# Router tokens turned by transfers and VectorE, token stores ahead of the slots' part, and a new written-out order

## The chip, the cores and the metric

The kernel runs on one core of one Trainium2 chip. The metric is the device time of one execution in microseconds (us); for the kernel before it is the median of three runs. All data are fp32. TensorE is called PE (its weight loads PEld), VectorE DVE, ScalarE ACT, GpSimd POOL, and the queue that issues most transfers SP.

## What is computed

The input x is 32 sequences of 512 tokens of 256 features. Two blocks follow each other, both with a residual.

- Attention: x is normalised; from it come a charge q (one number per token, tanh), a shell vector (64, scaled to length 1) and values. cos and sin of a projection of the shell, times the powers q^0 to q^4, are combined into phi (64). The weights are softmax(phi phi^T times a decay by distance), causal; x becomes x + weights @ values @ W_out.
- Slots (the feed-forward part), on the x that attention left:

```
xm    = layernorm(x)
h     = gelu(xm @ w1x.T + (part of the slots' mean) + b1)
alpha = softmax over the 8 largest of (h @ w2.T + b2), 0 for the other 56 slots
gi    = sum over tokens of alpha * xm / sum of alpha        # one row per slot
S'    = GRU(gi, slots)                                      # 64 slots per sequence
out   = x + alpha @ (S' @ wv.T + bv) @ wo.T + bo
```

## The kernel before, in words

The 32 sequences are taken two at a time: 16 groups of 2 sequences, of 8 token tiles of 128 tokens. For each group the code records steps (`add`): an engine, a cost, a function that emits the instructions, the steps it comes after, and the buffers it uses. Nothing is emitted while recording. At the end `Plan.order` places all steps of all groups one by one: it gives each a rank (from its place along the group's chain, the group's number times `STRIDE`, and a `DELAY` for each stage) and takes the step that could start first by the recorded costs, with the lower rank first among equals. Steps of several groups are mixed in this way. Each engine then runs its instructions strictly in that written-out order, SP's and POOL's transfers too. `SLOTS_OF` says how many buffers of each kind there are (x: 5 buffers of 8 tiles).

The stages of a group, with the lines of the kernel before:

1. load: `load_x` loads the tokens x twice, once as tokens (2 transfers of 512 KB) and, from group 2 on, once in 32x32 blocks as xb (8 transfers of 128 KB, L276).
2. tokens: `columns` turns xb into xT on DVE (L843, four 32x32-block transposes per group; groups 0 and 1 by PE, L821); `statistics` (DVE L753, POOL L764 to L774); `project` (PE L873) gives pf, DVE L886 scales it into sv.
3. angles: charges, shells, then five products tp: sine on ACT (L1042), two multiplications on DVE and two on POOL (`power`, all of them L1053).
4. phi (PE L1073, DVE L1088), then for the tiles (0,1), (2), (3): logits (PE L1127), their smallest with the mask (DVE L1156), exponent (ACT L1168), the weights turned (PE L1205, ACT L1223), values (PE L1211), and the sum onto x in place (DVE L1240).
5. normal: `statistics` again (POOL takes about 4 us for its part), xm on ACT (L1263, eight instructions of 128x256). `transposed` turns xm: 16 PE transposes of 128x128 (L789) into PSUM, four ACT copies of 128x512 out of it (L801).
6. router: hidden (PE L1290), gelu (ACT L1301), logits (PE L1315, turned in L1321), the 8 largest (DVE L1346 and L1347, eight times), softmax, al (POOL L1380).
7. taken, gru: psi (PE L1404), gi, the GRU's gates (PE L1454), small steps on DVE, ACT and POOL.
8. given: alpha turned (PE L1525), values of the slots (PE L1542), py (PE L1562). DVE adds py onto x in place (L1576, four of 128x512), and SP stores the tile pairs (L1581, four transfers of 256 KB). Until then the group holds its x buffer.

Of the kernel before, what the change touches and what calls it, by code (L numbers as in the profile page):

```python
# [15 lines left out]
P = 128  # L16
D = 256
# [6 lines left out]
SQ = 32  # L24
BY_TENSOR = 2
SHELL = 64
# [28 lines left out]
    "x": 5,  # L55
    "xb": 2,
    "xT": 4,
    "xmT": 4,
# [8 lines left out]
    "row": 8,  # L67
    "half": 5,
# [3 lines left out]
HOP = 0.28  # L72
TABLE = 1.28
SWITCH = 0.78
STRIDE = 36.18
LATE = 0.64
# [3 lines left out]
    "load": (14.7, 32.3),  # L80
    "tokens": (-16.4, 4.9),
    "angles": (-28.4, -6.2),
    "phi": (36.8, 9.6),
    "weights": (6.0, -2.0),
    "values": (-3.0, -21.2),
    "normal": (-19.3, -7.3),
    "router": (38.2, 2.0),
    "taken": (14.1, 0.1),
    "gru": (-28.5, -3.9),
    "given": (10.5, 2.0),  # L90
# [152 lines left out]
def block_kernel(ctx: ExitStack, tc: tile.TileContext, a: dict, out: bass.AP):  # L243
# [46 lines left out]
    def load_x(g, after=()):  # L290
        xs[g] = lazy("x", f"x_{g}", [P, GT, D])
        x_in[g] = []
        for bb in range(GB):

            def dst(g=g, bb=bb):
                return xs[g]()[:, bb * NT : (bb + 1) * NT, :]

            x_in[g].append(
                load("SP", dst, x[g * GB + bb].rearrange("(c p) d -> p c d", p=P), 512, after, [xs[g]])
            )  # L300
        if g < BY_TENSOR:
            return
        for bb in range(GB):
            xb = xbs[g, bb] = lazy("xb", f"xb_{g}_{bb}", [P, T // SQ, KD * SQ])
            blocks = x[g * GB + bb].rearrange("(t i) (q e) -> q i t e", i=SQ, q=P // SQ)
            xb_in[g, bb] = [
                load(
                    "SP",
                    lambda q=q, xb=xb: xb()[q * SQ : (q + 1) * SQ, :, :],
                    blocks[q],  # L310
                    128,
                    after,
                    [xb],
                    rate=150.0,
                )
                for q in range(P // SQ)
            ]
# [32 lines left out]
    xms = [const(f"xm{i}", [P, GT, D + 1]) for i in range(SLOTS_OF["xm"])]  # L350
# [165 lines left out]
    for q in range(P // SQ):  # L516
# [102 lines left out]
    def make_mask():  # L619
# [17 lines left out]
        lambda: [nc.gpsimd.memset(xm[:, :, D : D + 1], 1.0) for xm in xms],  # L637
# [6 lines left out]
    l_w1x = load("SP", w1x, rows(a["w1_t"][0:D, :]), 128, rank=30.0)  # L644
    l_w1s = load("SP", w1s, rows(a["w1_t"][D : 2 * D, :]), 128, rank=30.0)
# [133 lines left out]
    def transposed(g, n, src, uses, after, tag):  # L779

        res = {}
        for bb in range(GB):
            for k in range(KD):
                pt = bank(f"pt{n}_{g}_{bb}_{k}")
                dst = lazy(tag, f"{tag}_{g}_{bb}_{k}", [P, T])

                def turn(bb=bb, k=k, pt=pt):
                    for c in range(NT):
                        nc.tensor.transpose(  # L789
                            pt()[:, c * P : (c + 1) * P],  # L790
                            src()[:, bb * NT + c, k * P : (k + 1) * P],
                            ident,
                        )

                s = add(
                    "PE", 0.44, turn, after[bb * NT : (bb + 1) * NT] + [s_ident], uses + [pt, dst]
                )
                s = add(
                    "ACT",
                    0.54,  # L800
                    lambda dst=dst, pt=pt: nc.scalar.copy(dst(), pt()),  # L801
                    [s],
                    [pt, dst],
                )
                res[bb, k] = (dst, s)
        return res

    def columns(g, xt):
# [3 lines left out]
        for bb in range(GB):  # L812
# [25 lines left out]
            else:  # L838
                for h in range(2):
# [12 lines left out]
                    done.append([add("DVE", 0.6, turn, xb_in[g, bb], [xbs[g, bb], dst])])  # L852
# [3 lines left out]
    def features(g):  # L856
# [9 lines left out]
        for t in range(GT):  # L866
# [4 lines left out]
            def project(c=c, pf=pf, tile_=tile_):  # L871
                for k in range(KD):
# [12 lines left out]
                    0.42,  # L885
# [40 lines left out]
        qb = lazy("row", f"qb_{g}", [P, T])  # L926
        q2 = lazy("row", f"q2_{g}", [P, T])

        def charges_turned():
# [7 lines left out]
        s = add("PE", 0.44, charges_turned, s_rep + [s_ident], [qrep, ptq, qb])  # L937
        s_qb = add(
            "ACT", 0.6, lambda: nc.scalar.activation(qb(), ptq(), AF.Tanh), [s], [ptq, qb], "exp"
        )  # L940
        s_q2 = add(
            "ACT", 0.6, lambda: nc.scalar.activation(q2(), qb(), AF.Square), [s_qb], [qb, q2]
# [58 lines left out]
        tp = small(f"tp_{g}", [P, ORDER + 1, T], bufs=1)  # L1001
# [30 lines left out]
        def nearest():  # L1032
# [5 lines left out]
        s_tp = {}  # L1038
        s_tp[0] = add(
            "ACT",  # L1040
            0.6,
            lambda: nc.scalar.activation(tp()[:, 0, :], turn(), AF.Sin, scale=-TWO_PI),  # L1042
            [s],
            [turn, tp],
            "sin",
        )

        def power(eng, cost, m, by, s_by):
            e = nc.vector if eng == "DVE" else nc.gpsimd
            s_tp[m] = add(  # L1050
                eng,
                cost,
                lambda: e.tensor_tensor(  # L1053
                    tp()[:, m, :], tp()[:, m - 1 if by is qb else m - 2, :], by(), ALU.mult
                ),
                [s_tp[m - 1 if by is qb else m - 2], s_by],
                [tp, by],
            )

        power("DVE", 0.75, 1, qb, s_qb)  # L1060
        power("POOL", 1.2, 2, q2, s_q2)
        power("DVE", 0.75, 3, q2, s_q2)
        power("POOL", 1.2, 4, q2, s_q2)
# [4 lines left out]
        def combined():  # L1068
# [13 lines left out]
            "PE", 2.3, combined, list(s_tp.values()) + [s_wc], phs + [tp, phi], split="64x64"  # L1082
# [19 lines left out]
    def attention(g, sv, s_sv, phi, s_phi):  # L1102
# [147 lines left out]
        return s_x  # L1250

    def router(g, s_x):

        xt = xs[g]
        plan.stage = "normal"
        xm = Lazy("xm", lambda: xms[g % len(xms)])
        al = lazy("al", f"al_{g}", [P, NT, GB, SLOTS])
        ln, s_ln = statistics(g, "b", xt, [xt], s_x)
        s_xm = [
            add(  # L1260
                "ACT",
                0.51,
                lambda t=t: nc.scalar.activation(  # L1263
                    xm()[:, t, 0:D],
                    xt()[:, t, :],
                    AF.Identity,
                    bias=ln()[:, 4, t : t + 1],
                    scale=ln()[:, 1, t : t + 1],
                ),
                [s_ln, s_one],  # L1270
                [xm, xt, ln],
            )
            for t in range(GT)
        ]
        xm_t = transposed(g, "b", xm, [xm], s_xm, "xmT")
# [7 lines left out]
        for bb in range(GB):  # L1283
            ph = bank(f"ph_{g}_{bb}")
            h_t = lazy("h_t", f"h_t_{g}_{bb}", [H, T])
            tiles = [xm_t[bb, k][0] for k in range(KD)]

            def hidden(ph=ph, tiles=tiles):
                for k in range(KD):
                    nc.tensor.matmul(  # L1290
                        ph(), w1x[:, k, :], tiles[k](), start=(k == 0), stop=(k == KD - 1)
                    )

            s = add(
                "PE", 1.72, hidden, [xm_t[bb, k][1] for k in range(KD)] + [l_w1x], tiles + [ph, h_t]
            )
            s_h.append(
                add(
                    "ACT",
                    0.6,  # L1300
                    lambda ph=ph, h_t=h_t: nc.scalar.activation(h_t(), ph(), AF.Gelu, bias=b1e),  # L1301
                    [s, s_b1e],
                    [ph, h_t],
                    "gelu",
                )
            )
            h_ts.append(h_t)
# [35 lines left out]
        for t in range(GT):  # L1343
# [5 lines left out]
            s_top.append(add("DVE", 0.38, taken, [s], [rl, rest, top]))  # L1349
# [40 lines left out]
        return xm, al, s_al  # L1390

    def slots(g, xm, al, s_al):
# [7 lines left out]

        def taken_in():
            for c in range(NT):
                for bb in range(GB):
                    nc.tensor.matmul(  # L1404
                        psi()[bb * SLOTS : (bb + 1) * SLOTS, 0 : D + 1],
                        al()[:, c, bb, :],
                        xm()[:, bb * NT + c, :],
                        start=(c == 0),
                        stop=(c == NT - 1),
                    )  # L1410

        def amounts():
            nc.vector.tensor_scalar(rw(), psi()[:, D : D + 1], 1e-8, None, ALU.add)
# [3 lines left out]
        s_gi = add(  # L1417
            "DVE", 0.38, lambda: nc.vector.tensor_copy(gi(), psi()[:, 0:D]), [s_psi], [psi, gi]
        )
# [133 lines left out]
        )  # L1553
        for c2 in range(NT // 2):
# [15 lines left out]
            s = add("PE", 0.95, given, [s_val, s_alt], pys + [al_t, val], split="64x128")  # L1570
            for bb in range(GB):
                t = bb * NT + 2 * c2
# [7 lines left out]
                def stored(bb=bb, c2=c2, t=t):  # L1580
# [8 lines left out]
                add("SP", 0.8, stored, [s_y], [xt], land=2.0)  # L1589

    for g in range(NG):
# [6 lines left out]
        s_x = attention(g, sv, s_sv, phi, s_phi)  # L1598
        xm, al, s_al = router(g, s_x)
        slots(g, xm, al, s_al)  # L1600
# [63 lines left out]
```

## Time and profile before

| what | us |
|---|---|
| median of 3 runs (lowest, highest) | 727.66 (727.29, 728.21) |
| profiled execution, its own time | 729.78 |
| span in the profile, first to last instruction | 728.0 |
| one group in the even middle of the span (start of L1073 of one group to that of the next) | 42.27 |

The profile is of one execution, so its own time, 729.78, lies 2.1 us above the median; what is worked out from it is a difference, and is taken off the median. In the profile's rows a group of instructions is given by line, engine, operation, out<-in, sizes and count, then busy time, mean ns of one and idle time before. PE instructions are pipelined: the time that one takes on the engine is the distance from its start to the next one's start, which is shorter than its printed duration (a 128x128 transpose: 109 ns apart, 276 ns long). DVE instructions overlap likewise, by some 70 ns.

In the first 46 us PE is idle for 11.4 us (loads and weights), in the last 45 us for 13.7 us; between them it is idle for 4.8 us in all.

### The profile page before, as it was taken

The page shows a single profiled execution, that of the slowest core. Times are in us where ns is not written, and L with a number is a line of the kernel's source. Part 1 is how long each engine was busy: PE and PEld are TensorE (multiplying, and loading weights), DVE is VectorE, ACT ScalarE, POOL GpSimd, SP SyncE. Part 2 cuts the span into 40 slices and gives each one's busy share as a digit, 9 for nine tenths or more (in the row PEclk, how much of TensorE's full clock was granted, in tenths as well). Part 3 has the DMA queues.
Part 4 walks back from the last instruction along what each step waited for, and adds up shares of the span by engine and source line. Part 5 has one row for each costly group of instructions (what it writes and reads, how often), then busy time and mean ns, then how long its engine had stood idle before and what let it go on. Part 6 is the DMA issues. An engine that isn't in the chain of part 4 may idle for free.

```text
span 728.0 us, 12427 instructions
## 1 busy us (share of the span) xinstructions
PE 698.1 (96%) x4170; PEld 484.4 (67%) x4170; DVE 598.6 (82%) x1747; ACT 419.8 (58%) x866; POOL 268.3 (37%) x510
## 2 busy tenths in 40 slices
PE   4989999999999999999999999999999999999975
PEld 3747675777676767667676766767677667667443
DVE  3889978699797979889797988979797968768574
ACT  2335666846484765647476564747656582967631
POOL 6361624244151624425152442515243433231220
PEclk9999999999999999999999999999999999999989
DMA  6865422033333041333304123330410301000113
GB/s 143 265 119 140 73 45 59 1 117 59 116 58 117 8 109 59 59 117 59 116 14 103 59 59 116 59 116 21 97 58 1 116 1 59 1 1 1 58 43 132
DMA packets 99151, 53.76 MB, mean 74 GB/s; under 512 B 63088, under 2 KB 98256, under 8 KB 99088
## 3 DMA queue, kind: packets, MB, share of 16 engines
q1 hardware_dynamic: 97216, 52.02, 28.0%
q0 software_dynamic: 496, 0.33, 0.4%
q8 instruction: 33, 0.54, 0.3%
q10 hardware_dynamic: 1376, 0.62, 0.3%
q14 instruction: 30, 0.25, 0.1%
HBM read 35.85 MB, written 16.78 MB: 72 GB/s over the span
## 4 chain that ended last, share of the span: by engine, by line
PE 62%; DVE 27%; ACT 3%; POOL 3%; DMA 2%; issue 2%; SPq 1%; ACTq 0%; DVEq 0%; POOLq 0%
PE po L1211 15%; PE ph L1290 7%; DVE sv L886 6%; PE ptp L1205 5%; PE pl L1127 5%; PE prz L1454 4%; PE pf L873 4%; PE py L1562 4%; PE pph L1073 4%; DVE rest L1347 3%; DVE bnb L753 3%; DVE x L1240 3%; PE psi L1404 2%; PE prr L1315 2%; PE pv L1542 2%; DVE top L1346 2%
## 5 line engine op out<-in xcount | busy, mean ns | idle before, releaser
L1211 PE MATMUL po<-sv,prT 128*128 128x256 f32 x640 | 148.6, 381 | 1.1 <-DVE nm L1156 1.1
L1211 PEld LDWEIGHTS po<-sv,prT 128*128 128x128 f32 x640 | 116.8, 189 | 18.5 <-ACT prT L1223 1.3
L873 PE MATMUL pf<-wfb,xT 128*128 128x321 f32 x448 | 125.6, 436 | 0.0
L873 PEld LDWEIGHTS pf<-wfb,xT 128*128 128x128 f32 x448 | 83.3, 189 | 38.0 <-issue 4.5
L1263 ACT ACTIVATE xm<-x,lnb 128x256 f32<-128x256 f32 x128 | 64.6, 587 | 29.6 <-POOL lnb L774 29.6
L1168 ACT ACTIVATE pr<-lg,nm 128x512 f32<-128x512 f32 (+3 forms) x128 | 70.9, 555 | 7.4 <-DVE nm L1156 5.9
L1053 POOL TENSOR_TENSOR tp<-tp,q 128x512 f32<-128x512 f32 x32 | 48.9, 1528 | 68.8 <-ACT tp L1042 67.5
L1240 DVE SCALAR_TENSOR_TENSOR x<-po,den,x 128x256 f32<-128x256 f32 x128 | 60.2, 474 | 13.5 <-PE po L1211 13.1
L764 POOL TENSOR_TENSOR lnb<-bnb 128x8 f32<-128x8 f32 x16 | 3.3, 208 | 179.0 <-DVE bnb L753 179.0
L1156 DVE CUSTOM_DVE_ANT_0 lg<-pl,mask 128x512 f32<-128x512 f32 (+3 forms) x128 | 57.0, 484 | 9.1 <-PE pl L1127 8.6
L886 DVE SCALAR_TENSOR_TENSOR sv<-pf,lna,bias_f 128x321 f32<-128x321 f32 x128 | 62.0, 538 | 2.7 <-POOL lna L770 2.5
L1290 PE MATMUL ph<-xmT,w1x 128*128 128x512 f32 x128 | 60.9, 602 | 0.0
L1364 ACT ACTIVATE rl<-rl,rtau 128x512 f32<-128x512 f32 x16 | 11.6, 723 | 83.1 <-DVE rl L1355 83.1
L1576 DVE TENSOR_TENSOR x<-py,x 128x512 f32<-128x512 f32 x64 | 39.9, 683 | 21.3 <-PE py L1562 21.3
L753 DVE BATCH_NORM_STATS2 bnb<-x 128x6 f32<-128x256 f32 x128 | 54.1, 426 | 3.7
L1223 ACT COPY prT<-ptp 128x384 f32<-128x384 f32 (+1 forms) x96 | 46.1, 513 | 18.1 <-PE ptp L1205 18.1
L753 DVE BATCH_NORM_STATS2 bna<-x 128x6 f32<-128x256 f32 x128 | 47.1, 413 | 6.9 <-DMA x<-in_x_dram 6.9
L1205 PE MATMUL ptp<-ident,pr 128*128 128x128 f32 x320 | 46.7, 277 | 0.0
L1127 PE MATMUL pl<-phi 64*128 64x256 f32 (+1 forms) x384 | 46.4, 364 | 0.0
L1205 PEld LDWEIGHTS ptp<-ident,pr 128*128 128x128 f32 x320 | 36.3, 140 | 13.7 <-issue 6.0
L1073 PE MATMUL pph<-tp,wc 64*64 64x256 f32 x640 | 38.9, 381 | 0.2 <-POOL tp L1053 0.2
L1127 PEld LDWEIGHTS pl<-phi 64*128 64x128 f32 x384 | 30.3, 186 | 12.4 <-issue 8.9
(177 smaller groups left out, 1338.3 us busy)
## 6 DMA issues: line engine op xcount, KB each, us to landing
x<-in_x_dram SPq DMA_DIRECT2D x32, 512.0 KB, 5.1
out_dram<-x SPq DMA_DIRECT2D x64, 256.0 KB, 2.5
xb<-in_x_dram SPq DMA_DIRECT2D x112, 128.0 KB, 3.5
setup<-in_gru_whh_t_dram SPq DMA_DIRECT2D x1, 768.0 KB, 5.7
wih<-in_gru_wih_t_dram SPq DMA_DIRECT2D x1, 768.0 KB, 6.8
wfb<-wf SPq DMA_DIRECT2D x8, 40.1 KB, 5.2
setup<-in_W_v_dram ACTq DMA_DIRECT2D x1, 256.0 KB, 9.0
setup<-in_W_out_t_dram ACTq DMA_DIRECT2D x1, 256.0 KB, 9.0
```

The lines of the kernel that those rows point to most:

```text
L753: lambda t=t: nc.vector.bn_stats(st()[:, t, :], src()[:, t, :]),
L873: nc.tensor.matmul(pf()[:, 0:NF], tile_()[:, k, c * P : (c + 1) * P], w[:, k, :], start=(k == 0), stop=(k == KD - 1),)
L886: lambda t=t, pf=pf: nc.vector.scalar_tensor_tensor(sv()[:, t, :], pf()[:, 0:NF], ln()[:, 1, t : t + 1], bias_f, ALU.mult, ALU.add,),
L1073: nc.tensor.matmul(phs[h]()[bb * COMB : (bb + 1) * COMB, 0:HT], wc[r, m, :], tp()[r, m, bb * HT : (bb + 1) * HT], start=(m == 0), stop=(m ...
L1127: nc.tensor.matmul(pls[bb]()[:, off[i] + lo : off[i] + lo + w], phi()[r, 0, q : q + P], phi()[r, 1, k : k + w], start=True, stop=True,)
L1156: nc.vector.tensor_tensor_reduce(out=lg()[:, c], in0=pls[bb]()[:, c], in1=mask[:, T - w : T], scale=1.0, scalar=TOP, op0=ALU.add, op1=ALU.min,
L1168: nc.scalar.activation(pr()[:, c], lg()[:, c], AF.Exp, bias=nm(), scale=-1.0, accum_out=den()[:, tiles.index(i), bb : bb + 1],)
L1205: nc.tensor.transpose(pt()[:, j : j + P], prs[bb]()[:, j : j + P], ident)
L1211: nc.tensor.matmul(po()[:, d * D : (d + 1) * D], pr_t()[:, lo : lo + P], sv()[:, bb * NT + j, C_V:NF], start=(j == 0), stop=(j == i),)
L1240: nc.vector.scalar_tensor_tensor(xt()[:, t, :], po()[:, d * D : (d + 1) * D], den()[:, d, bb : bb + 1], xt()[:, t, :], ALU.mult, ALU.add,)
L1263: lambda t=t: nc.scalar.activation(xm()[:, t, 0:D], xt()[:, t, :], AF.Identity, bias=ln()[:, 4, t : t + 1], scale=ln()[:, 1, t : t + 1],),
L1290: nc.tensor.matmul(ph(), w1x[:, k, :], tiles[k](), start=(k == 0), stop=(k == KD - 1))
```

## The change

- Router tokens: for groups 0 to 13 the 16 PE transposes and four ACT copies go. xm is laid out as [128, 4 quarters of 64 features, 8 tiles, 64 + 1]; 32 transfers by SP (16 per sequence, each of 32 partitions x 1,040 bytes, SBUF to SBUF) put blocks where they belong, and four DVE transposes in 32x32 blocks finish it, in place (xmT). The hidden matmul reads the new layout with rows of w1 in another order (w1b, four more loads at the start); gelu writes its output back into the order of tokens. Groups 14 and 15 turn by PE as before.
- Stores: for groups 0 to 14, SP stores x (2 transfers of 512 KB) as soon as attention is done. ACT copies py out of PSUM into ys (four of 128x512), and POOL issues two transfers of 512 KB that add ys onto what was stored. DVE's four additions of 128x512 go. Group 15 is as before.
- Powers: two DVE multiplications of 128x1024 take the place of two of 128x512 on DVE and two on POOL; q and q^2 lie in the same tile.
- Buffers: x 5 to 4, xT 4 to 3, xmT 3 of another shape, row 8 to 6, half 5 to 4; new: ys 2.
- Ranks: `HOP`, `SWITCH`, `STRIDE`, `LATE`, every `DELAY` and some costs have new values, so the written-out order is another one on every engine.

```diff
-    "x": 5,
+    "x": 4,
...
+    "ys": 2,
+    "row": 6,
+    "half": 4,
...
-HOP = 0.28
+HOP = 0.41
-SWITCH = 0.78
-STRIDE = 36.18
-LATE = 0.64
+SWITCH = 1.41
+STRIDE = 11.97
+LATE = 0.85
...
-    "normal": (-19.3, -7.3),
-    "router": (38.2, 2.0),
-    "taken": (14.1, 0.1),
-    "gru": (-28.5, -3.9),
-    "given": (10.5, 2.0),
+    "normal": (-37.6, -17.2),
+    "router": (-0.8, -0.4),
+    "taken": (-20.0, -22.0),
+    "gru": (4.0, 0.6),
+    "given": (-0.8, -23.8),
...
-        power("DVE", 0.75, 1, qb, s_qb)
-        power("POOL", 1.2, 2, q2, s_q2)
-        power("DVE", 0.75, 3, q2, s_q2)
-        power("POOL", 1.2, 4, q2, s_q2)
+        for m in (1, 3):
+
+            def powers(m=m):
+                a, b = tp()[:, 0:1, :], tp()[:, ORDER + 1 : ORDER + 3, :]
+                if m == 1:
+                    a = a.to_broadcast([P, 2, T])
+                else:
+                    a, b = tp()[:, 1:3, :], b[:, 1:2, :].to_broadcast([P, 2, T])
+                nc.vector.tensor_tensor(tp()[:, m : m + 2, :], a, b, ALU.mult)
+
+            s_tp.append(add("DVE", 1.3, powers, [s_tp[-1], s_q], [tp]))
...
+        if g < NG - LAST_BY_VECTOR:
+
+            for bb in range(GB):
+
+                def store(bb=bb):
+                    nc.sync.dma_start(
+                        out=out[g * GB + bb].rearrange("(c p) d -> p c d", p=P),
+                        in_=xt()[:, bb * NT : (bb + 1) * NT, :],
+                    )
+
+                stored.append(
+                    add("SP", 1.7, store, s_x[bb * NT : (bb + 1) * NT], [xt], land=3.0)
+                )
...
+                moved = [
+                    add(
+                        "SP",
+                        0.45,
+                        lambda bb=bb, q=q, b=b, dst=dst: nc.sync.dma_start(
+                            out=dst()[q * SQ : (q + 1) * SQ, b * NT : (b + 1) * NT, :],
+                            in_=xm()[b * SQ : (b + 1) * SQ, q, bb * NT : (bb + 1) * NT, :],
+                        ),
+                        here,
+                        [xm, dst],
+                        land=2.3,
+                    )
+                    for b in range(NT)
+                    for q in range(NQ)
+                ]
+                for h in range(2):
+
+                    def turn(h=h, dst=dst):
+                        n = NT * NT // 2
+                        v = dst()[:, h * n : (h + 1) * n, 0:EQ]
+                        nc.vector.transpose(v, v)
+
+                    done.append(add("DVE", 0.63, turn, moved, [dst]))
...
+                    s_ys[bb].append(add("ACT", 0.54, kept, [s], [pys[bb], ys[bb]]))
...
+            def accumulate(bb=bb):
+                nc.gpsimd.dma_start(
+                    out=out[g * GB + bb].rearrange("(c p) d -> p c d", p=P),
+                    in_=ys[bb](),
+                    accum_op=ALU.add,
+                )
+
+            add("POOL", 1.2, accumulate, s_ys[bb] + [stored[bb]], [ys[bb]], land=5.0)
```

## The prediction

> **What bounds the kernel now.** First I read the page's busy times, then the busy times by window, then one group's stretch in the timelines.
>
> ```profile
> PE 698.1 (96%) x4170; PEld 484.4 (67%) x4170; DVE 598.6 (82%) x1747; ACT 419.8 (58%) x866; POOL 268.3 (37%) x510
> ```
>
> PE is idle for 728.0 - 698.1 = 29.9 us of the span. The windows (length, then busy PE, PEld, DVE, ACT, POOL, granted clock, DMA share, GB/s) tell where:
>
> ```profile
> 0.00:46.00 46.00, 34.58 (x146) 25.21 (x146) 29.65 (x79) 14.57 (x24) 25.09 (x59) 1.00 0.79 195
> 227.69:269.95 42.26, 42.18 (x260) 29.35 (x262) 36.47 (x109) 25.48 (x54) 15.94 (x30) 1.00 0.30 76
> 683.00:728.00 45.00, 31.34 (x160) 18.41 (x158) 27.94 (x92) 13.45 (x25) 6.40 (x8) 0.91 0.24 82
> ```
>
> In a group of the even middle (42.26 us) PE is idle for 0.08 us, DVE for 5.8. So PE's work sets the middle; the start (11.4 us idle) and the last group's chain (13.7) are set by latency. DVE isn't far behind, and the chain of waits of a middle group shows that it is no bystander:
>
> ```profile
> 443.29 0.24 DVE top L1346
> ...
> 459.14 0.32 DVE gi L1418
> 459.46 0.07 DVE rw L1413
> 459.54 0.42 PE pt_gi L1428 x2
> ```
>
> For 16 us the chain runs along DVE while PE is full beside it. Both engines stand near the bound there, so PE time that goes is worth its full size only if DVE gets its own work into the shorter group.
>
> **PE: the transposes go.** In the PE timeline (start, then length, line, count) the two blocks of 8 take, start to next start, 456.02 - 455.06 = 0.96 and 458.84 - 457.91 = 0.93:
>
> ```profile
> 455.06 1.03 PE L789 MATMUL ptb<-ident,xm 128*128 128x128 f32 x8
> 456.02 1.96 PE L1404 MATMUL psi<-xm,al 128*64 128x257 f32 x16
> 457.91 1.09 PE L789 MATMUL ptb<-ident,xm 128*128 128x128 f32 x8
> 458.84 0.60 PE L1525 MATMUL pta<-ident,al 128*128 128x128 f32 x4
> ```
>
> 1.89 us per group, in 14 groups 26.5 us. psi gets 260 columns for 257: 1.2% of 1.89, 0.3 us in 14 groups. The hidden matmul has as many columns, read 32 at a time; the trace has no such read of PE's. Bounds: nothing, or as much as a change of operand costs at the edge of a block (0.96 less 8 x 0.109 = 0.09) for each of its 8 instructions, 0.7 us per group. I take nothing, since psi and pf read their operands with steps now and run at their size. PE then needs 42.27 - 1.87 = 40.40 us.
>
> **DVE: does it fit into 40.40?** From its timeline:
>
> ```profile
> 463.11 1.30 DVE L843 STREAM_TRANSPOSE xT<-xb 128x512 f32<-128x512 f32 x2
> ...
> 472.95 0.68 DVE L1053 TENSOR_TENSOR tp<-tp,qb 128x512 f32<-128x512 f32 x1
> 473.66 1.64 DVE L1053 TENSOR_TENSOR tp<-tp,q 128x512 f32<-128x512 f32 x1
> ...
> 479.44 2.48 DVE L1576 TENSOR_TENSOR x<-py,x 128x512 f32<-128x512 f32 x4 [1.86 <-PE py L1562]
> ```
>
> - The four additions of py go: -2.48, and the 1.86 of waiting ahead of them.
> - Four transposes come, of the shape of L843: 2 x 1.30 = +2.60 at most.
> - Powers: 0.68 + 1.64 = 2.32 go. The second is slow because POOL multiplies at the same time (L1053 on POOL, 3.12 us for two from 471.63). Two of 128x1024 come: 4 x 0.68 = 2.72 undisturbed, 4 x 1.64 = 6.56 with POOL reading throughout. POOL's share of these products is gone, but in the new order its al (1.04 us) stands beside one of them and can take (1.64 - 0.68) / 1.56 of its length, 0.65. So 2.7 to 3.4; I take 2.7.
>
> Sum: 36.5 - 2.48 + 2.60 - 2.32 + 2.72 = 37.0 us busy. Its waits now, 5.8 us, lose the 1.86 for py; 1.20 before phi (for pph L1073) are filled in the new order by nn and bna, which stand there. 2.7 remain: 39.7, some 0.7 us under PE's 40.40. PE stays the bound, barely.
>
> **The transfers that turn the tokens** are a new wait: DVE's transposes wait for 16 transfers each half, and DVE's whole queue stands behind them. SP's issues of xb take 4.33 us for 8, 0.53 apart. The nearest transfer of the kind is wfb, 32 partitions x 1,284 bytes, SBUF to SBUF:
>
> ```profile
> L276 SPq DMA_DIRECT2D wfb<-wf x8: 507/582/603, 17.7 to 24.4; - x8
> ...
> DMA to landing us min/median/max: 1.8/5.2/6.8
> ```
>
> The upper values are from the start, where DMA is 0.79 busy; in the middle it is 0.30 and will be about half. A group's first half is ready, counted from its last po: x and bnb 0.85, POOL's statistics 4.1, four xm 2.0, two stores 1.06, 16 issues 8.5, landing 1.8 to 6.8: 18.3 to 23.3 us. In the new order PE does prz, psi, ph, pt_gi, pn, pph, pta, pf, pl and prr in between, 23.8 us by today's distances: no wait. The second half is ready at 26.8 to 31.8; its turn stands 4.6 us of PE's work later, at 28.4: a wait of 0 to 3.4 us. I take the landing near 2 to 3 us (hs, 64 KB on SP: 2.8): none. PE needs the result only 11.7 us later (ph). In all SP issues 44 transfers per group, 23 us of 40: loads behind the moves are not late, and 4 x buffers do, since x is free after xm and the store, no longer after py.
>
> The Trainium skill ("DMA: Bandwidth & Descriptors", "Rules for kernel authors") speaks against these moves: many small transfers should be one large one, under 64 KB mostly overhead is paid. Its fit (section "Anatomy of one DMA") gives an estimate of 2.1 us for 33 KB; by that there is no wait, by the row's median of 5.2 there is one of 1.8 us in DVE's queue. The skill also ("VectorE: DVE Perf Modes", "Rules for kernel authors") sends a 128x128 transpose to TensorE. By the 311 ns of its table for a (bf16) block on VectorE, 16 blocks would be 5.0 us, DVE would stand at 42.1 and nothing would be won; L843's row says 2.6.
>
> **What costs nothing.** ACT: four copies of 128x512 out of PSUM go (L801), four of the same size come (ys); it is busy 25.5 of 42. Two more table loads (51 to 53, 1.28 each) fall into its idle time. POOL loses 3.1 us and gets two issues of adding transfers. The trace has no such issue: bounds 0.54 (om) and 2.8, wc's 0.69 for 320 rows times four; I take 1, POOL has 26 us idle. Their landing: 2.6 to 8.1 (POOL's transfers at the start). It delays only ys's next use, a group later, and the end: py of group 14 starts 12.6 us before the end now, and 1.93 + 4 x 0.48 + 2 + 8.1 = 14.0 is at most 1.4 us past it; below, DVE's four additions (2.5 us) leave the last stretch, but py of group 15 waits for PE. I take 0.
>
> **Start and end.** The order there is much the same: ptb, ph, psi, prz, py of group 15 follow each other as now. Four more loads of w1 (0.63 each) stand ahead of x of group 1, but the load of whh leaves that place. I take 0, with 3 us to either side.
>
> **Sum.** 14 x 1.87 = 26.2 us. Of the profiled execution's 729.78 that leaves 703.6; of the median, 2.1 lower, 701.5. DVE's slack falls from 5.8 to some 3, so I let PE's idle time double to 0.16 per group, 1.1 us: **702.6**, by itself 698 to 708. Chance 45%.
>
> **Rivals.**
> - DVE becomes the bound (28%). It keeps all 3.9 us of waits and loses 0.65 in the powers: 37.0 + 0.65 + 3.9 = 41.6, so 0.7 x 14 = 10 us won: **718** (708 to 722). For: the chain of 16 us. Against: those waits are mostly DVE being early.
> - The new order alone also helps (12%): each change of the kind of matmul costs PE 0.1 to 0.16 (psi: 1.89 for 16 x 0.108); pl now stands together more often. Three fewer per group: 0.4 x 16 = 6 us: **696**, to 694.
> - The transposes were hidden (5%): DVE's 16 us stretch sets the group as before: **726**.
> - Slower (10%): the moves land late because the 1 MB store stands just ahead of them in SP's queue and the adding transfers run beside them. From a landing of 6.6 us DVE stands at 37.0 + 2.0 (half its waits) + 3.2 = 42.2 and the gain is gone; at 8.1 (om's) the wait is 4.7: 43.7, 1.5 x 14 = 21 more: **748**. For: wfb's 6.8. Against: DMA is busy half the time at most.
>
> Range 696 to 721: it leaves out about 5% below and 15% above. Under 0.2% can't be told from no change here; faster 0.85, same 0.04, slower 0.11.
>
> **What would show it.** Groups 40.4 to 40.6 us apart at pph; no ptb for 14 groups; PE idle under 0.3 us per group; DVE about 37 busy; the new transposes waiting for nothing; moves landing within 3 us. Wrong, if DVE waits long at the new transposes, if POOL's adding issues take several us, or if PE is idle in the first groups.

## The result, and the profile after

The changed kernel takes **780.49 us** (median of 4 runs, 775.6 to 783.32), the kernel before beside it 727.93 (4 runs, 727.29 to 729.59): a ratio of 1.0711, with an interval of 1.0654 to 1.0769. It is slower, outside the range of the forecast. The profiled execution of after took 779.99 us, 50.2 more than that of before; the spans, 778.2 and 728.0, differ by the same 50.2.

The page of after, in the order in which the page of before was read: busy times, then the shares of the chain that ended last, the new transposes and the adding issues among the costly groups (busy, mean ns | idle time before, what ended it), and two kinds of DMA issue (KB each, median us to landing):

```profile
PE 689.1 (89%) x3946; PEld 468.1 (60%) x3946; DVE 595.1 (76%) x1743; ACT 422.4 (54%) x871; POOL 291.6 (37%) x510
...
SPq 28%; PE 23%; DVE 20%; POOL 10%; DMA 6%; ACT 5%; issue 5%; DVEq 0%; ACTq 0%; POOLq 0%
...
L1348 DVE STREAM_TRANSPOSE xmT<-xmT 128x512 f32<-128x512 f32 x56 | 39.4, 706 | 89.1 <-DMA xmT<-xm 81.7
...
L1688 POOL DMA_DIRECT2D out_dram<-ys x30 | 40.4, 1525 | 79.5 <-ACT ys L1661 78.9
...
out_dram<-ys POOLq DMA_DIRECT2D x30, 512.0 KB, 7.2
...
xmT<-xm SPq DMA_DIRECT2D x448, 32.5 KB, 1.9
```

PE's busy time fell, but its share fell from 96% to 89%, and the chain, which was 62% PE before, is led by SP's queue (SPq 28%). Now the window of one group, from one pph to the next (length, then busy PE, PEld, DVE, ACT, POOL, granted clock, DMA share, GB/s):

```profile
374.06:419.22 45.16, 40.40 (x236) 28.01 (x235) 36.67 (x106) 26.24 (x54) 17.06 (x30) 1.00 0.55 118
```

PE is busy for 40.40 us and DVE for 36.67 in this group. The forecast had 40.40 and 37.0. (DVE's 36.67 is typical: the eight windows from pph to pph between 190.76 and 557.90 have a mean of 36.63. PE's 40.40 is the low side of 40.31 to 42.12, mean 41.39, at a mean clock of 0.95.) But the group lasts 45.16 us, not 40.4. Idle time appeared, on PE (4.8 us) and on DVE (8.5, where 2.7 was forecast).

What DVE and PE stood still for (us in total, times, longest), from the waits of after:

```profile
DVE xmT L1348 <- DMA xmT<-xm: 81.7, 29, 7.3
POOL out_dram L1688 <- ACT ys L1661: 78.9, 10, 16.8
...
PEld psi L1482 <- POOL al L1454: 35.1, 13, 5.9
...
PE psi L1482 <- POOL al L1454: 27.5, 11, 5.1
```

DVE waits 81.7 us for the moves, some 5.8 per group, and PE waits in front of psi. The chain of waits shows how the two hang together (start, us, what):

```profile
355.48 3.88 DMA xmT<-xm
...
359.49 0.71 DVE xmT L1348
...
369.30 0.44 DVE bnb L763
...
369.80 1.11 POOL lnb L774
...
375.55 0.25 POOL lnb L784
...
376.33 0.76 ACT xm L1282 x2
...
377.93 0.51 SPq L1332
...
397.71 0.58 SPq L1332
398.30 0.05 issue
398.34 1.83 DMA xmT<-xm
...
400.45 0.71 DVE xmT L1348
```

This is **a loop that closes once per group**: one turn leads from a group's last transpose to the next group's. The late transpose at 359.49 holds up what stands behind it in DVE's queue: the next group's x and its statistics (bnb), which end at 369.74, 10.2 us later. Then POOL's statistics (6.0), ACT's first xm (2.1), 32 issues by SP (20.4), a landing (1.8): the next group's last transpose at 400.45, again late. Nothing in this turn is PE. It is 41.0 us long; the one before it, from 307.98 to 359.49, is 51.5. There DVE does 14.2 us of work up to the last bnb, and between POOL's statistics and ACT's xm stand POOL's al and PE's psi, so that the first issue starts 4.2 us after the statistics instead of 2.1:

```profile
328.40 0.24 POOL lnb L784
328.64 1.02 POOL al L1454
329.70 1.54 PE psi L1482 x11
331.25 0.48 ACT xm L1282
```

POOL's statistics take 6.4, the row of issues 22.6 (the last one 2.08), the landing 3.9. So the long turns carry more than SP's row. Long and short turns mostly alternate; from the last transpose of group 2 to that of group 13 (175.45 to 675.97) it is 45.5 per group, against 42.27 from pph to pph before.

SP's timeline of the same stretch (start, length from the first start to the last end, line, count):

```profile
377.93 21.00 SPq L1332 DMA_DIRECT2D xmT<-xm  x32
399.03 1.07 SPq L281 DMA_DIRECT2D x<-in_x_dram  x2
400.52 5.84 SPq L281 DMA_DIRECT2D xb<-in_x_dram  x8
413.35 1.25 SPq L1244 DMA_DIRECT2D out_dram<-x  x2
```

The moves' issues follow each other at 0.63 us, and both sequences' moves stand in one row: 20.4 us from first to last issue. The prediction had 0.53, from the issues of xb; the written-out order was made with 0.45.

PE's timeline shows one more cost (start, us, ..., idle time before):

```profile
358.04 1.88 PE L1538 MATMUL prz<-wih,giT 128*128 128x512 f32 x4
364.99 3.74 PE L1482 MATMUL psi<-xm,al 128*64 128x260 f32 x16 [5.07 <-POOL al L1454]
368.66 4.39 PE L1370 MATMUL ph<-xmT,w1b 128*128 128x512 f32 x8
```

After 5.07 us of idle time psi takes 3.74 us for what takes 1.9 otherwise. The window of that psi shows a granted clock of 0.50 (columns as above):

```profile
364.99:368.66 3.67, 3.67 (x17) 1.73 (x17) 3.53 (x9) 1.91 (x2) 0.00 (x0) 0.50 0.59 113
```

PE goes on at half speed for a while. In this execution the mean granted clock is 0.955, before 0.992.

**Where the 50.2 us come from.** An experiment below (e3) runs the same 3946 PE instructions with no idle gap in the middle: 668.9 us busy. Taken as the measure of undisturbed work, it says that PE lost 698.1 - 668.9 = 29.2 us of work, did what is left 689.1 - 668.9 = 20.2 us slower, and is idle for 89.1 us instead of 29.9: -29.2 + 20.2 + 59.2 = 50.2.

### The profile page after: what moved, and what is told of

Its sections match the earlier page's. It is cut to its first block, busy times and chain, and to the rows that moved or that the text cites. A ratio compares the mean times of both kernels' runs of the same rounds, so it can differ in the third digit from the quotient of the medians.

```text
span 778.2 us, 12771 instructions
## 1 busy us (share of the span) xinstructions
PE 689.1 (89%) x3946; PEld 468.1 (60%) x3946; DVE 595.1 (76%) x1743; ACT 422.4 (54%) x871; POOL 291.6 (37%) x510
## 3 DMA queue, kind: packets, MB, share of 16 engines
q0 software_dynamic: 16336, 16.06, 14.2%
## 4 chain that ended last, share of the span: by engine, by line
SPq 28%; PE 23%; DVE 20%; POOL 10%; DMA 6%; ACT 5%; issue 5%; DVEq 0%; ACTq 0%; POOLq 0%
SPq L1332 28%; PE pf L854 7%; DVE bnb L763 5%; DVE x L1227 5%; DMA xmT<-xm 4%; PE po L1198 3%; PE psi L1482 2%; POOL lnb L780 2%; ACT xm L1282 2%; PE pl L1114 2%; DVE turn L1026 2%; PE py L1648 2%; ACT pr L1155 1%; POOL lnb L774 1%; DVE rest L1421 1%
## 5 line engine op out<-in xcount | busy, mean ns | idle before, releaser
L854 PE MATMUL pf<-wfb,xT 128*128 128x321 f32 x448 | 129.6, 437 | 0.4 <-DVE x L1227 0.4
L1198 PEld LDWEIGHTS po<-sv,prT 128*128 128x128 f32 x640 | 116.4, 189 | 19.2 <-issue 1.9
L1348 DVE STREAM_TRANSPOSE xmT<-xmT 128x512 f32<-128x512 f32 x56 | 39.4, 706 | 89.1 <-DMA xmT<-xm 81.7
L867 DVE SCALAR_TENSOR_TENSOR sv<-pf,lna,bias_f 128x321 f32<-128x321 f32 x128 | 66.6, 540 | 12.9 <-PE pf L854 9.7
L1688 POOL DMA_DIRECT2D out_dram<-ys x30 | 40.4, 1525 | 79.5 <-ACT ys L1661 78.9
L1454 POOL TENSOR_TENSOR al<-rl,asum 128x512 f32<-128x512 f32 x16 | 18.2, 1140 | 128.6 <-DVE asum L1447 128.6
L1370 PE MATMUL ph<-xmT,w1b 128*128 128x512 f32 x112 | 59.8, 676 | 5.7 <-DVE xmT L1348 5.7
L1482 PE MATMUL psi<-xm,al 128*64 128x260 f32 (+1 forms) x256 | 40.2, 467 | 27.5 <-POOL al L1454 27.5
L941 POOL TENSOR_TENSOR sq<-sv 128x256 f32<-128x256 f32 x32 | 20.2, 633 | 90.8 <-DVE sv L867 88.4
L1482 PEld LDWEIGHTS psi<-xm,al 128*64 128x64 f32 x256 | 20.1, 162 | 47.5 <-POOL al L1454 35.1
L1114 PE MATMUL pl<-phi 64*128 64x256 f32 (+1 forms) x384 | 42.2, 355 | 2.7 <-ACT giT L1520 2.5
```

Source lines behind the costliest of these rows:

```text
L854: nc.tensor.matmul(pf()[:, 0:NF], tile_()[:, k, c * P : (c + 1) * P], w[:, k, :], start=(k == 0), stop=(k == KD - 1),)
L867: lambda t=t, pf=pf: nc.vector.scalar_tensor_tensor(sv()[:, t, :], pf()[:, 0:NF], ln()[:, 1, t : t + 1], bias_f, ALU.mult, ALU.add,),
L1114: nc.tensor.matmul(pls[bb]()[:, off[i] + lo : off[i] + lo + w], phi()[r, 0, q : q + P], phi()[r, 1, k : k + w], start=True, stop=True,)
L1198: nc.tensor.matmul(po()[:, d * D : (d + 1) * D], pr_t()[:, lo : lo + P], sv()[:, bb * NT + j, C_V:NF], start=(j == 0), stop=(j == i),)
L1370: nc.tensor.matmul(ph(), w[:, k, :], rhs, start=(k == 0), stop=(k == KD - 1))
L1482: nc.tensor.matmul(psi()[bb * SLOTS : (bb + 1) * SLOTS, 0:width], al()[:, c, bb, :], plain()[:, t, :] if plain else xm()[:, :, t, :], star ...
```

## The experiments

Each label has one kernel, run beside the kernel before (727.7 to 729.6 us) on the same chip: one execution each, four for e11 and e12. The kernel of e3 took 702.0 to 707.7 us in five executions, after 775.6 to 783.3 in four, so a few us between single runs tell nothing. Three theories are named in the expectations. **A:** the order was written with too short an issue time for the moves, so DVE's transposes stand too early in its queue and the loop through SP's queue sets the distance of the groups. **B:** POOL's adding transfers cause it. **C:** the new ranks are poor as such.

**e1, all groups turn by PE.** No moves; the stores, the adding transfers, the powers and the new ranks stay.

```diff
-LAST_BY_TENSOR = 2
+LAST_BY_TENSOR = 16
```

> One part undone: all 16 groups turn the router's tokens by PE and ACT, none by transfers; stores, adding transfers, powers, buffers and ranks stay new. Theory A (the loop of a group runs through SP: 32 issues of 0.63 us, 20 us, between ACT's xm and DVE's turned tokens, and DVE's next additions and statistics stand behind that turn): the loop is gone, PE has 26 us of transposes back, so about 730, 720 to 740, groups 42 to 43 apart. Theory B (POOL's adding transfers, 1.5 us of issue each and 16 MB more to move, cost the time): still 770 or more. Theory C (the new ranks make a poor order whatever the transfers do): 760 or more.

Measured: 719.88 us. PE is busy for all of the 200 us from 300 to 500, and its 4170 instructions, as many as before, take 688.1 us in all:

```profile
PE 688.1 (96%) x4170; PEld 481.9 (67%) x4170; DVE 561.6 (78%) x1687; ACT 452.4 (63%) x928; POOL 276.7 (39%) x524
```

So what turned the change slower came with the moves. Without the moves the other parts together are 7.8 us faster than the kernel before beside it (727.71), 0.1 under the range of theory A. From pph to pph a middle group takes 41.7 us (211.68 to 587.14, nine groups), where theory A had 42 to 43.

**e2, after's order without the adding transfers.** The slots' part is then missing from the output of groups 0 to 14.

```diff
             def accumulate(bb=bb):
-                nc.gpsimd.dma_start(
-                    out=out[g * GB + bb].rearrange("(c p) d -> p c d", p=P),
-                    in_=ys[bb](),
-                    accum_op=ALU.add,
-                )
+                return None
```

> The adding transfers are left out, so the slots' part is missing from the output of groups 0 to 14; the written-out order of everything else is the changed kernel's. Theory A: 770 to 781, since POOL's 40 us of issues and the traffic are not what the group waits for. Theory B: the loss is gone, 725 to 740. Theory C: 775 or more.

Measured: 756.95 us, and DVE still waits 71.3 us for the moves. Both pure theories missed: without the adding transfers 23 us go, so in this order the adding transfers cost something, but they aren't the main cause: 29 us over before stay. The run takes away POOL's issues (1.53 us each, where the order reckons with 1.2), the 78.9 us of waiting for ys ahead of them and their 16 MB of traffic together, so it doesn't show which of them costs.

**e3, the order written with the measured issue time.** The only edit is the cost by which the planner orders; the instructions are the same.

```diff
                         "SP",
-                        0.45,
+                        0.64,
                         lambda bb=bb, q=q, b=b, dst=dst: nc.sync.dma_start(
```

> Only the planner's cost of one move is changed, 0.45 to 0.64 us, which is what SP takes on the chip; so the same instructions are written out in another order, in which DVE's turns stand later. Theory A: DVE's 82 us of waiting for moves falls under 30, and the time to 715 to 745. Theory B: 770 or more, since POOL's work is the same. Theory C: 765 or more, since the ranks are the same.

Measured: 705.31 us, 75 less than after. Busy times, and the wait that was 81.7:

```profile
PE 668.9 (95%) x3946; PEld 460.3 (65%) x3946; DVE 593.9 (84%) x1743; ACT 423.2 (60%) x871; POOL 287.6 (41%) x510
```

```profile
DVE xmT L1348 <- DMA xmT<-xm: 3.2, 4, 1.8
```

PE is not idle at all between 300 and 500 us, and the groups are 39.4 apart (177.85 to 532.06 at pph, nine groups, columns as above):

```profile
177.85:532.06 354.21, 354.01 (x2136) 244.69 (x2135) 327.63 (x960) 229.50 (x476) 157.95 (x270) 1.00 0.61 132
```

The moves still take 20.2 to 23.5 us per group in SP's queue, from the first start to the last end; only, the transposes now stand where their data have landed, from just in time to some 3 us later.

**e4, 16 moves of twice the size.** Each carries both sequences (32 partitions x 2,080 bytes) and waits for all eight xm; a group has one xmT, of which there are 2; lg and pr lose a buffer each; the cost is 0.64.

```diff
-                            out=dst()[q * SQ : (q + 1) * SQ, b * NT : (b + 1) * NT, :],
-                            in_=xm()[b * SQ : (b + 1) * SQ, q, bb * NT : (bb + 1) * NT, :],
+                            out=dst()[q * SQ : (q + 1) * SQ, b, :, :],
+                            in_=xm()[b * SQ : (b + 1) * SQ, q, :, :],
                         ),
-                        here,
+                        s_xm,
```

> Each move takes both sequences of the group (32 partitions x 2,080 bytes), so 16 moves for 32 in a group; cost 0.64 in the planner; xmT 2 buffers of double size, paid with lg 2 for 3 and pr 4 for 5. A move now waits for all eight xm. Theory A: the loop is 16 x 0.63 = 10 us shorter, less 2 us for the later start: PE bounds the group again, 41 us, in all 700 to 720. Theory B and theory C: 760 or more.

Measured: 704.80 us, a wait of 1.3 us. Half the issues bring nothing over e3: where the order fits, SP's time is covered either way. The rule weighed in the prediction, that small transfers are mostly overhead, agrees with the landings (65 KB in 2.0 us, 33 KB in 1.9), but that overhead is not what cost the time: with half as many transfers it is the same.

**e5, half of the moves issued by ACT, in after's order.**

```diff
-                        lambda bb=bb, q=q, b=b, dst=dst: nc.sync.dma_start(
+                        lambda bb=bb, q=q, b=b, dst=dst: (nc.scalar if q % 2 else nc.sync).dma_start(
```

> The order of every engine is that of the changed kernel, but every second move (odd quarter) is issued by ACT instead of SP: 16 of the 32 issues of a group leave SP's queue. Theory A (the time that SP takes for the issues, 32 x 0.63 = 20.4 us of the loop of 45 us, sets the distance of the groups): SP's part of the loop falls to 10.2 us, the loop to some 35 to 38 us, below PE's 40.4, and DVE's wait for the moves (81.7 us) falls below 25; the issues on ACT (16 x 0.63 = 10 us on 27 of 45) give some of it back: 710 to 745, say 725. Theory B (POOL's adding transfers are the cause): the wait stays above 60 and the time at 765 to 785. Theory C (the new ranks as such are poor, whatever the moves): no change, 775 to 785.

Measured: 778.29 us, where theory A had 725: a clear miss of the number. DVE's own wait for the moves is gone (0.2 us), as theory A had it, but the time is the one that B and C expected, and DVE now waits for ACT:

```profile
DVE den L1180 <- ACT pr L1155: 37.0, 21, 3.8
DVE lg L1143 <- ACT pr L1155: 31.7, 21, 4.4
```

ACT's queue is in order too, and the issues stand in it among the softmax's exponentials, which DVE and PE need; the order had kept no time for them there. The test replaced one late queue by another and doesn't tell the theories apart. The Trainium skill ("DMA: Bandwidth & Descriptors", section "Issuing engines are not separate DMA queues") says that issuing from several engines "will only save the time on the sequencer it takes to initiate the DMA, which is usually small relative to the DMA itself". For one move this holds in part, 0.63 against 1.9 to landing. But the landings overlap and the issues don't: 32 x 0.63 = 20 us per group stood in the row. Moving half of them saved nothing here, since this order kept no place for them in ACT's queue.

**e6, e9, e10: orders written with 0.53, 0.60 and 0.70 us for a move**, otherwise e3's edit.

> The order is written with 0.53 us for the issue of a move, the distance that the prediction took, instead of 0.45; all instructions are the same. Theory A: 32 x 0.08 = 2.6 us of the 5.8 us that the order leaves out per group are now in it; the turns still stand too early by 32 x 0.10 = 3.2 us per half-pair: DVE's wait for the moves is between 3 and 82 us, and the time between the two known orders (705.3 and 780.5): 725 to 765, say 745. Theory C (the time depends on which order the planner happens to find, not on the issue time): no relation, 700 to 790.

> The order written with 0.60 us for the issue of a move (its measured distance is 0.63); all instructions are the same. Theory A: only 32 x 0.03 = 1 us per group is left out, little more than the slack of the turns: DVE's wait for the moves under 20 us, 703 to 725, say 710. Theory C (each order is a matter of luck, and 0.64 was a lucky one): no relation to the cost, anywhere from 700 to 790.

> The order written with 0.70 us, more than an issue takes; all instructions are the same. Theory A: above 0.63 nothing is left out any more, so the wait stays under 8 us and PE is the bound: 700 to 712. Theory C: no relation, 700 to 790.

| cost in the order, us | 0.45 (after) | 0.53 | 0.60 | 0.64 (e3) | 0.70 |
|---|---|---|---|---|---|
| time, us | 780.0 | 750.7 | 721.0 | 705.3 | 713.5 |
| DVE's wait for the moves, us | 81.7 | 41.7 | 11.1 | 3.2 | 1.9 |
| PE idle from 300 to 500 us | 22.7 | 9.5 | 3.6 | 0.0 | 1.2 |

The time falls as the cost nears the measured 0.63, as theory A expects. With 0.60 it was 11 us more than the number given, within the range; with 0.70 1.5 us above the range. An issue thought too long is harmless for the moves (1.9 us of waiting), yet another wait is then left over. That an order is a matter of luck to some 10 us is not excluded by these runs; that it explains 75 is.

**e7, e3 without the adding transfers** (e2's edit and e3's).

> The order written with 0.64 us for the issue of a move (705.3 us), with the adding transfers of POOL left out (the slots' part is missing from the output of groups 0 to 13). Theory A: in an order that knows the issue time POOL isn't in a loop, and the adding transfers are hidden: 700 to 706, at most 5 us less. Theory B (the adding transfers cost some 23 us in any order): 680 to 690, which PE's busy 668.9 us would allow.

Measured: 698.26 us, 7.05 less than e3, between the two theories, and 3.8 below the lowest of the five executions of e3's kernel. (The slots' part is missing from the output of groups 0 to 14; the expectation says 13.) 2.3 us of it lie ahead of the last group's pph (610.62 against 612.89), 4.8 after it. So of the 23 us of e2 some two thirds belonged to the poor order.

**e8, after with the old ranks.** `HOP`, `SWITCH`, `STRIDE`, `LATE` and every `DELAY` as before:

```diff
-STRIDE = 11.97
+STRIDE = 36.18
...
-    "router": (-0.8, -0.4),
+    "router": (38.2, 2.0),
...
```

> The changed kernel's steps, with the ranks of the kernel before in place of the new ones (the planner finds another order; 0.45 us for a move stays). Theory A: the order still believes in 0.45 us, so DVE still waits for the moves (over 40 us) and the time is 745 to 790. Theory C (the new ranks are the cause): the wait is small and the time 700 to 730.

Measured: 821.32 us, with a wait for the moves of 49.1. Theory C is contradicted: the old ranks are 41 us worse for these steps. It is also 31 us above theory A's range; this order has further waits (POOL's nn, ACT's pr), which weren't taken apart.

**e13 and e14, e3's order with a longer SP queue.** The runs that speak for theory A so far (e3, e6, e9, e10) change the order together with the cost, and e5, which kept it, had failed. So the good order was kept and only SP's issue time made longer, by spare transfers of 1 KB whose data nothing reads.

```diff
+    spares = const("spares", [SQ, 16, 8])
+
+    def spare(k):
+        nc.sync.dma_start(out=spares[:, k, :], in_=ident[0:SQ, 0:8])
...
+                            q == 0 and spare(bb * NT + b + 8 * (q // 2)),
```

(e14 has `q % 2 == 0`.)

> The order written with 0.64 us for a move (704.8 us), unchanged on every engine, with 8 spare transfers of 1 KB per group (each 32 partitions x 32 bytes, to a place that nothing reads), one behind every fourth move in SP's queue. Theory A (SP's issue time stands in the loop that sets the distance of the groups, and what the order doesn't know of it is paid in full beyond a small slack): 8 x 0.63 = 5 us per group, less a slack of some 1.5 us (of the 6.1 us that 0.45 leaves out, 4.6 showed in the distance of the groups): 3.5 x 13 = 46 us more, 750 (735 to 770), with DVE's wait for the moves at 30 to 65 us. Rival (SP, issuing 23 of 40 us, has room, and 0.45, 0.53 and 0.60 only happened to give poor orders): under 712, no wait.

> The same with 16 spare transfers per group, one behind every second move. Theory A: 10 us per group less 1.5, 8.5 x 13 = 110 us more: 815 (780 to 835). Rival: under 720.

Measured: 775.38 and 852.50 us. Busy times and the wait of e13, then those of e14 (L1356 is L1348 of after):

```profile
PE 691.2 (89%) x3946; PEld 466.5 (60%) x3946; DVE 593.9 (77%) x1743; ACT 423.7 (55%) x871; POOL 287.5 (37%) x510
```

```profile
DVE xmT L1356 <- DMA xmT<-xm: 70.0, 20, 7.2
```

```profile
PE 715.1 (84%) x3946; PEld 477.9 (56%) x3946; DVE 595.4 (70%) x1743; ACT 423.7 (50%) x871; POOL 287.7 (34%) x510
```

```profile
DVE xmT L1356 <- DMA xmT<-xm: 145.4, 30, 10.5
```

8 issues, 5.1 us per group, cost 70.1 us over e3's 705.31; 16, 10.1 us, cost 147.2: 5.0 and 10.5 us in each of 14 groups. The slack of 1.5 us that the expectations took off didn't show, so both lie above the ranges given. The distance of the groups says the same. From the last transpose of group 2 to that of group 13 it is 39.9 us in e3, 45.3 in e13 and 50.8 in e14: 5.4 and 10.9 more. That is a little more than the issues themselves; PE's slower work after idle time (691.2 us busy for 668.9 in e13) is in it, not separated. After has 45.5, which is 5.6 more than e3, and what its order leaves out is 32 x (0.63 - 0.45) = 5.8; its wait (81.7) and PE's busy time (689.1) are near those of e13, too. Nor is SP's queue simply full. In e13 it issues for some 39 of the 45 us between two groups' first moves:

```profile
359.33 2.10 SPq L281 DMA_DIRECT2D x<-in_x_dram  x2
361.53 7.64 SPq L281 DMA_DIRECT2D xb<-in_x_dram  x8
369.27 1.66 SPq L1249 DMA_DIRECT2D out_dram<-x  x2
376.30 0.51 SPq L1338 DMA_DIRECT2D xmT<-xm  x1
```

(The row of moves and spares ahead of these lines lasts from 331.12 to 358.92.) Before 376.30 it stands still for 5.4 us, and yet what was added is paid in full. With the order held, this shows theory A's loop: time that SP takes and the order doesn't know of is paid once per group.

**e11 and e12, the best order timed.** e11 is e3 again; in e12 group 14, too, adds on DVE and is stored in four pieces.

```diff
-LAST_BY_VECTOR = 1
+LAST_BY_VECTOR = 2
```

> The kernel whose order was written with 0.64 us for the issue of a move, again, for its interval: 703 to 708 beside some 728, a ratio of 0.966 to 0.972.

> The order written with 0.64 us, and group 14 adds its slots' part on DVE and stores it in four pieces, as the kernel before does; groups 0 to 13 keep the adding transfers. In the trace with 0.64 the last adding transfers are issued 11 us before the end, on the heels of PE's last instructions, and the run ends 9.3 us after PE, 6.1 in the kernel before. If they set the end: 2 to 4 us less, 701 to 703. If the end is set otherwise (the last group's stores): 704 to 707; if DVE's four additions (2.5 us) delay the last group's chain: 706 to 709.

Measured: e11 704.75 us (4 runs, 702.01 to 707.65), a ratio to before of 0.9672 (0.964 to 0.9704); e12 704.88 (703.52 to 705.05), 0.9667 (0.9649 to 0.9685). e12 is no faster: either the last adding transfers don't set the end, or what is saved there is lost at the four additions; the runs don't tell which. Both beat the kernel before by 3.3% and the change as it stands by nearly 10%.

## Why the prediction was wrong, point by point

- **PE's term, 26.2 us: near in sum, with luck in it.** Over the whole span 29.2 us of PE's work went (698.1 to e3's 668.9). But e1, which keeps the PE transposes, has 688.1: 10.0 of the 29.2 came with the other parts of the change, and 19.2 with the moves. In the even middle it looks different again: 42.27 us per group before, 41.72 in e1, 39.36 in e3, so there the way without PE's transposes brings some 2.4 for the 1.87 forecast. The 40.40 of the one window of after is a coincidence: in e3, where PE is never idle in the middle, the work is 39.4.
- **DVE's busy time: right.** 36.67 for 37.0 (mean of eight groups 36.63); the powers take 2 x 1.21 = 2.4 us (2.7 forecast), the transposes 4 x 0.71 printed. POOL's 128x8 statistics beside a power grew from 0.2 to 1.1 and 1.3 us, while the prediction looked for contention beside al only (beside al a power took 1.54 at most, 0.33 more, where 0.65 was weighed).
- **The failed step: "16 issues 8.5", and "a wait of 0 to 3.4 us", taken as "none".** Two things failed in it. First the size: an issue of a move takes 0.63, not the 0.53 of xb's; 16 take 10.1, and a group's 32 stand in a row for 20.4. (So SP's "23 us of 40" was too low as well: in the group shown it is some 29 of 45.) Second, the kind. The wait was priced as something that happens within one group, at most 3.4 us, and covered by PE's distances of today. But DVE's queue behind the transpose holds the next group's x and bnb, from which the next moves start: the delay comes back. What the order doesn't know of is paid in every group, as e13 and e14 show. The number that told it stood in the diff: the order was written with 0.45 per move, and the prediction itself held 0.53 in its hand; 32 x 0.08 = 2.6 us per group of it were visible, and e6 shows what an order with that much in it is worth: 750.7 instead of 780.0.
- **The landing, 2 to 3 us taken: right** in the median (1.9; at most 6.4, and 3.9 in the long turn above). The 2.1 us that the prediction worked out by the fit of the Trainium skill ("DMA: Bandwidth & Descriptors", section "Anatomy of one DMA") lies close, too, though the page gives that fit for transfers issued by GpSimd and these are issued by SP. The rival that ends slower, 748, had asked for landings over 6.6 us; that condition was not met, and the loss came from elsewhere. It had the place right: DVE's queue stands behind the transposes.
- **The adding transfers, 1 us per issue and 0 in all: too small.** 1.53 per issue; the median landing of 7.2 lies within the 2.6 to 8.1. "It delays only ys's next use, a group later, and the end" left out that POOL's issue waits for ys (78.9 us) with al and lnb behind it in POOL's queue. Without the transfers 23 us go in after's order and 7 in e3's; that it is this wait that costs them is not shown.
- **PE's clock: not in the prediction.** After idle time, the largest wait of which is the one for al in front of psi (27.5 us), PE ran slower; its busy time is 20.2 us above e3's for the same instructions. Here a stall cost more than its length.
- **The forecast of 702.6 is what the change brings with an order that knows the issue time** (e3 and e11: 705.3 and 704.75). That isn't a success of the prediction: it took for granted that the written-out order fits the costs as they are on the chip.
- **A small misreading:** the table loads of ACT are 53 before and 54 after, not 51 and 53. Nothing in the sum rests on them.

Left open: why e1's PE needs 10 us less than before for as many instructions (the rival of 696 had 6 us for fewer changes between kinds of matmul; that wasn't tested), what in the adding transfers costs the 23 us of e2, and the last 10 us between orders that all fit the moves.

## What to carry to other kernels

Where an order is written out by costs, compare each new cost in it with the distance of like issues in the trace, multiply by the count per period, and compare that with the slack of what waits. A wait in an in-order queue that also holds the start of the next round closes a loop: follow it once around, add up its legs, and compare the sum with the bound of the busiest engine, since what exceeds it is paid every time. And the busy share of a queue (here some 29 of 45 us in after) says nothing of whether its time lies in such a loop.

## What the runs showed of the hardware

- In these rows an issue on SP took 0.63 us from start to start (median), for transfers within SBUF of 1 KB (e13), 33 KB (after, e3) and 65 KB (e4) alike; single issues took up to 2.2 (e3). The issue of an adding transfer of 512 KB on POOL took 1.5.
- Small POOL operations stretch beside a large one of DVE. POOL's timeline of after, and DVE's beside it:

```profile
369.80 1.11 POOL L774 TENSOR_TENSOR lnb<-bnb 128x8 f32<-128x8 f32 x1 [4.87 <-DVE bnb L763]
...
371.33 1.34 POOL L777 TENSOR_SCALAR lnb<-lnb 128x8 f32<-128x8 f32 x1
...
376.37 0.21 POOL L774 TENSOR_TENSOR lna<-bna 128x8 f32<-128x8 f32 x1 [0.59 <-DVE bna L763]
```

```profile
369.64 1.21 DVE L1048 TENSOR_TENSOR tp<-tp 128x1024 f32<-128x1024 f32 x1
...
371.36 1.21 DVE L1048 TENSOR_TENSOR tp<-tp 128x1024 f32<-128x1024 f32 x1
```

  The same line of POOL takes 1.11 us while DVE's power runs (369.64 to 370.85) and 0.21 when it doesn't; both end within 0.1 us of DVE. The Trainium skill ("SBUF — State Buffer", "Who interferes with whom") has DVE and POOL share one pair of ports under an exclusive lock, and says that a DVE instruction with two SBUF inputs, as the power is, contends with a POOL instruction that reads SBUF. These rows agree. DVE, at 1.21 both times, pays nothing here; in before, beside long POOL products, it paid (1.64 for 0.68).
- After 5.07 us of idle time PE ran at half speed for psi and a part of ph (granted clock 0.50; 3.74 us for 1.9, then 4.39 for 3.8, the mean of e3's 14).
